# A two-layer graph attention kernel: the normalized input turned in 32 by 32 blocks on VectorE, and elu plus one with a single exponential

## The chip, the cores and the metric

The kernel runs on one core of a Trainium2 chip. The metric is the device time of one execution in microseconds (us), lower is better; where several runs were made it is their median. A core has five engines that run side by side, each through its own queue in a fixed order: TensorE (PE in the profile, with its weight loads as PEld), VectorE (DVE), ScalarE (ACT), GpSimd (POOL) and SyncE (SP), which here only issues DMAs. They wait for each other through semaphores. TensorE leaves its products in eight banks of its output memory (PSUM), which VectorE and ScalarE must empty ("drain").

## The reference

B = 32 batches, N = 512 nodes, 512 features, all in fp32; layer 1 has 4 heads of 256, layer 2 one head of 512.

```python
def gat_layer(x, mask, W, a_src, a_dst, bias, concat):
    xl = (x @ W).reshape(B, N, H, F)
    asrc = jnp.einsum('bnhf,hf->bnh', xl, a_src)
    adst = jnp.einsum('bnhf,hf->bnh', xl, a_dst)
    e = jax.nn.leaky_relu(asrc[:, :, None, :] + adst[:, None, :, :], NEG_SLOPE)
    e = jnp.where(mask[..., None], e, NEG_INF)
    attn = jax.nn.softmax(e, axis=1)
    out = jnp.einsum('bsdh,bshf->bdhf', attn, xl)
    out = out.reshape(B, N, H * F) if concat else out.mean(axis=2)
    return out + bias
...
mask = (adj > 0) | jnp.eye(N, dtype=bool)[None]
h = jnp.maximum(_layernorm(x, axis=-1), 0.0)
g = jax.nn.elu(gat_layer(h, mask, W1, att_src1, att_dst1, b1, concat=True))
return x + gat_layer(g, mask, W2, att_src2, att_dst2, b2, concat=False)
```

## The kernel before

`tile_gat` (L347) does not issue its work directly. It records jobs in a `Program` (from L101): each has an engine, a planned cost in us, and the keys it reads and writes. A list scheduler (`order`) then lays the jobs out. TensorE keeps the order in which the jobs were recorded; VectorE, ScalarE, GpSimd and SyncE are reordered by the planned costs and by what waits for a job. `emit` (L1525) issues the instructions in that order, so it is fixed before the kernel runs. All instructions pass through a few helpers, and so they share line numbers in the profile: `act` is L476, `dve` L479, `dma` on SyncE L482, GpSimd's adding DMA of the mask into `p` L487, `pe` L493; only SyncE's transposing DMAs have lines of their own, L637 (`mt<-m`) and L696 (`x<-adj`). Work is told apart by tile names.

The matrix products are done by a Strassen-Winograd scheme in seven half-size products instead of eight (`sevens`, L931, and `gather1`, L1146, for layer 1's weighted sum). Each product is named by a number n from 1 to 7, needs some sums of blocks on its left or right (VectorE: `hs<-ht`, `hs<-h`, `x<-xl`, `t<-p`), and leaves banks that are copied (ScalarE) or added (VectorE) into the result. A matrix product in fp32 takes two passes on TensorE.

A batch goes through these steps:

- `load` (L602) reads x in four tiles of 128 rows. `norm` (L645) takes mean and variance on VectorE. `norm_turn` (L665) does `x<-x,stats` (scale, shift and Relu in one ScalarE instruction) and turns the tile, since TensorE needs it with features on partitions (`ht`). For the first two batches TensorE turns it. For the 30 others ScalarE splits the fp32 words into 16-bit halves (`adj<-x`), SyncE issues a transposing DMA (`x<-adj`), and ScalarE puts the halves together (`ht<-x`).
- `project1` (L1028): `ht` times W1, as `mm<-w_sb,ht` and `mm<-w_sb,hs`, into `xl`, with the attention scores in extra columns.
- softmax of layer 1, over several steps: scores (`z`, `flip`), DMAs that spread them over partitions (`drr<-flip`, `rr<-drr`, `das<-flip`, `as<-das`), sums of exponentials (`l`, `low`), and `p`: VectorE writes it, GpSimd adds the mask (`p<-dm`), ScalarE takes the exponential (`p<-p,z`).
- `gather1` (L1146): `p` times `xl`, into `h`, transposed. The banks are copied into `h` by ScalarE (`h<-mm`) or added by VectorE. When a group is complete, `elu` (L1049) turns it into elu plus one, up to sign: ScalarE takes exp (`xr<-h,b_sb`), then a Relu (`xr<-xr`), and VectorE joins it with the bias (`h<-h,b_sb,xr`).
- `project2` (L1223): `h` times W2. Two of the seven products find `b2_sb` already in their banks, put there by ScalarE (`mm<-b_sb`).
- `gather2` (L1314), layer 2's weighted sum. `residual` reads x again (`t<-in_x_dram`) and the result leaves with `out_dram<-t`. Its sums on the right side (`sums2`, L1299) borrow two of the four x tiles.

The main loop (L1463) records for each batch i: `gather1` of batch i+1, heads 0 and 1; `project1` of batch i+2, first half; `gather1`, heads 2 and 3; `project1`, second half; `gather2` of batch i-1; `project2` of batch i+1; then `load`, `norm` and `norm_turn` of batch i+3. On TensorE the last two stand between each other's products where the recorder pairs them (`pipe`). Ahead of the loop, `weights2` (L555) loads W2, b1 and b2, and the first batches go through simpler versions (`project1_first`, `gather1_plain`, L1061).

Of the kernel before, what the change touches and what calls it, by code (L numbers as in the profile page):

```python
# [346 lines left out]
def tile_gat(  # L347
# [74 lines left out]
    AT = {(0, 0): 0, (0, 1): 6, (1, 0): 1, (1, 1): 2}  # L422
    b1_sb = sbuf.tile([P, 2, FT], F32, name="b1_sb")
    b2_sb = sbuf.tile([P, 2, W2H], F32, name="b2_sb")
    part = sbuf.tile([P, 2, FT, 2], F32, name="part")
    xl = sbuf.tile([P, NT, H, W], F32, name="xl")
# [4 lines left out]

    xs = slots("x", NT, [P, D])
    adj2 = sbuf.tile([P, 2, N], I32, name="adj2")
# [121 lines left out]
    def weights2():  # L555

        for (r, c), ix in AT.items():
            dma(
                1.5, [("ht", 0, 0)], [("w2", ix)], w2_sb[:, ix, :, :M],
                w2[r * HF // 2 : (r + 1) * HF // 2, c * DO // 2 : (c + 1) * DO // 2].rearrange(  # L560
                    "(k p) f -> p k f", p=P
                ),
            )
        dma(0.1, (), ["b1"], b1_sb[:, 0], b1.rearrange("(c p) -> p c", p=P))
        dve(TINY, ["b1"], ["b1"], nc.vector.tensor_scalar_mul, b1_sb[:, 1], b1_sb[:, 0], -1.0)
        dve(0.3, (), ["b2"], nc.vector.memset, b2_sb, 0.0)
        for c in range(2):
            dma(
                0.4, (), ["b2"], b2_sb[:, c, :M],
                bass.AP(tensor=b2.tensor, offset=b2.offset + c * M, ap=[[0, P], [1, M]]),  # L570
            )
        dve(0.34, ["b2"], ["b2"], nc.vector.tensor_sub, b2_sb[:, 1], b2_sb[:, 0], b2_sb[:, 1])
        dve(0.2, ["b2"], ["b2"], nc.vector.tensor_scalar_mul, b2_sb[:, 0], b2_sb[:, 0], -1.0)
        for a, v in enumerate((as2, ad2)):
            lk, bc = ts_.take()
            bc = bc[:, 0, :]
            dma(0.75, (), [lk], bc, rows_of(v[0], P))
            for (r, c), ix in AT.items():
                for k in range(KH):
                    jk, junk = xrs.take()  # L580
                    dve(
                        0.4, [lk, ("w2", ix)], [("part", a, r, c, k), jk],
                        nc.vector.scalar_tensor_tensor,
                        junk[:, : DO // 2], w2_sb[:, ix, k, :M], 1.0,
                        bc[:, c * DO // 2 : (c + 1) * DO // 2], op0=OP.mult, op1=OP.mult,
                        accum_out=part[:, a, r * KH + k, c : c + 1],
                    )
                    xrs.give(jk)
            ts_.give(lk)
        for a in range(2):  # L590
            for r in range(2):
                g = part[:, a, r * KH : (r + 1) * KH, :]
                dve(
                    TINY, [("part", a, r, c, k) for c in range(2) for k in range(KH)],
                    [("w2s", AT[r, a])], nc.vector.tensor_add,
                    w2_sb[:, AT[r, a], :, M:], g[:, :, 0:1], g[:, :, 1:2],
                )


    XT, MASK, MASKT, ST = {}, {}, {}, {}  # L600

    def load(b):  # L602
        XT[b] = []
        for t in range(NT):
            xk, xt = xs.take()
            dma(1.1, (), [xk], xt, x[b, t * P : (t + 1) * P, :])
            XT[b].append((xk, xt))

# [36 lines left out]
    def norm(b):  # L645
        sk, st = stats.take()
        S, A = nc.vector.BN_STATS_DIM, nc.vector.BN_AGGR_DIM
        for t, (xk, xt) in enumerate(XT[b]):
            dve(0.61, [xk], [sk + (t,)], nc.vector.bn_stats, st[:, t, :S], xt)
            dve(TINY, [sk + (t,)], [sk + (t,)], nc.vector.bn_aggr, st[:, t, S : S + A], st[:, t, :S])  # L650
# [14 lines left out]
    def norm_turn(b, t):  # L665

        (sk, st), (xk, hn) = ST[b], XT[b][t]
        S, A = nc.vector.BN_STATS_DIM, nc.vector.BN_AGGR_DIM
        act(
            0.71, [xk, sk + (t,)], [xk], hn, hn, AF.Relu,  # L670
            bias=st[:, t, S : S + 1], scale=st[:, t, S + A : S + A + 1],
        )
        if b < 2:
            pk, pt = banks.take()
            pe(
                [xk], [pk], 0.44,
                [(nc.tensor.transpose, (pt[:, k * P : (k + 1) * P], hn[:, k * P : (k + 1) * P], identf), {})
                 for k in range(KT)],
            )
            act(  # L680
                0.62, [pk], [("ht", t, 0), ("ht", t, 1)], ht[:, :, t * P : (t + 1) * P],
                pt.rearrange("p (k n) -> p k n", n=P), AF.Copy,
            )
            banks.give(pk)
        else:

            ak, a = adjs.take()
            words = a.bitcast(U16)
            act(
                0.96, [xk], [ak], words.rearrange("p (h f) -> p h f", h=2),  # L690
                hn.bitcast(U16).rearrange("p (f h) -> p h f", h=2), AF.Copy,
            )
            back = hn.bitcast(U16)
            prog.add(
                "SP", 1.3, [ak], [xk],
                lambda: nc.sync.dma_start_transpose(  # L696
                    back.rearrange("p (g n) -> p g n", n=P), words
                ),
                1.9,
            )  # L700
            act(
                1.21, [xk], [("ht", t, 0), ("ht", t, 1)],
                ht[:, :, t * P : (t + 1) * P].bitcast(U16).rearrange("p k (n h) -> p h k n", h=2),
                back.rearrange("p (h k n) -> p h k n", h=2, n=P), AF.Copy,
            )
            adjs.give(ak)
        xs.give(xk)
        if t == NT - 1:
            stats.give(sk)


    def p_keys(pk, us=range(NT), cs=range(2)):
# [195 lines left out]
    def ht_blocks():  # L908
        return half_blocks(ht, KQ, lambda r, c: [("ht", 2 * r, c), ("ht", 2 * r + 1, c)])

# [4 lines left out]

    def minus(to):

        def put(n, us, bks, ps, fresh):  # L920
            d, keys = to(us, *BLOCK[n - 1])
            if fresh:
                act(COPY2, bks, keys, d, ps, AF.Copy, scale=-1.0)
            else:
                dve(ADD2, bks + keys, keys, nc.vector.tensor_sub, d, d, ps)

# [72 lines left out]
    def project1_first(zt):  # L999

        for j in range(H // 2):
            zk, z = zt[j]
            for t in range(NT):
                for c in range(2):
                    h = 2 * j + c
                    bk, bt = banks.take()
                    pe(
                        [("ht", t, 0), ("ht", t, 1)]
                        + [q for r in range(2) for k in range(KQ)
# [18 lines left out]
    def project1(b, left, j):  # L1028
        def to(us, r, c):
# [6 lines left out]
        yield from sevens(  # L1036
            left, lambda n, u, k: w1_sb[:, n - 1, k, u[1], :], lambda n: w1_keys(n - 1), minus(to),
            KQ, [(m, j) for m in range(2)], W, LAST,
# [9 lines left out]

    def elu(g, places, at):  # L1049

        keys = [("h1", g, r) for r in range(2)]
        ek, e = xrs.take()
        act(0.62, [*places, "b1"], [ek], e, at, AF.Exp, bias=b1_sb[:, 0, g : g + 1], scale=-1.0)
        act(0.54, [ek], [ek], e, e, AF.Relu, bias=1.0, scale=-1.0)
        dve(
            0.65, [*places, ek, "b1"], keys, nc.vector.scalar_tensor_tensor,
            h1[:, g, :], at, b1_sb[:, 1, g : g + 1], e, op0=OP.add, op1=OP.min,
        )
        xrs.give(ek)

    def gather1_plain(soft, heads):  # L1061

        for h in heads:
            pk, p = soft.p.pop(h)
            for f in range(FPH):
                bk, ps = banks.take()
                for s in range(NT):
# [8 lines left out]
                    )  # L1076
                elu(h * FPH + f, [bk], ps)
                banks.give(bk)
            ps_.give(pk)
            yield h  # L1080
# [65 lines left out]
    def gather1(soft, order):  # L1146
# [11 lines left out]
        for u, n in order:  # L1158
# [27 lines left out]
            elif n in (2, 4, 5, 6):  # L1186
                act(COPY2 if two else COPY, bks, keys, to, ps, AF.Copy)
            else:
                dve(ADD2 if two else ADD, bks + keys, keys, nc.vector.tensor_add, to, to, ps)
            if n in (2, 3, 4):  # L1190
# [11 lines left out]
            if n in (3, 4):  # L1202
                for q in g:
                    elu(q, [("h1", q, x) for x in range(2)], h1[:, q, :])
            if n == 4:
# [17 lines left out]
    def project2(b, left, order=LAST):  # L1223
# [7 lines left out]
        def to(us, r, c):  # L1231
# [6 lines left out]
            left, lambda n, u, k: w2_sb[:, n - 1, k, :],  # L1238
            lambda n: [("w2", n - 1), ("w2s", n - 1)], minus(to), KH, [(0,), (1,)], W2H, order,
            {1: (b2_sb[:, 0], "b2"), 5: (b2_sb[:, 1], "b2")},  # L1240
        )

    def scores_2(b):
        def cols(z, i, zk):
            v = x2(b)
            for a in range(2):
                dve(
                    TINY, [x2_key(b, t, a) for t in range(NT)], [zk + (0, a)],
                    nc.vector.tensor_copy, z[:, a, 0, :], v[:, :, a * W2H + M],
                )  # L1250
# [35 lines left out]
    def sums2(b, soft, place=None, keys=None):  # L1286
# [12 lines left out]
        t1, t2 = (  # L1299
            (t.rearrange("p (k f) -> p k f", f=M), [k]) for k, t in (xs.take() for _ in range(2))  # L1300
        )
# [12 lines left out]
    def gather2(b, soft, blocks, order=LAST):  # L1314
# [27 lines left out]
        for n in (5, 6):  # L1342
            xs.give(right[n][1][0])

# [54 lines left out]
    S1, S2 = {}, {}  # L1399
    HT_KEYS = [("ht", t, c) for t in range(NT) for c in range(2)]  # L1400

# [35 lines left out]
    flush()  # L1437
    weights2()
    s = S1[1] = Soft(1, 1, scores_1)
    for h in gather1_plain(S1[0], range(H)):  # L1440
# [116 lines left out]
```

## Time and profile before

| what | value |
|---|---|
| median of 3 runs | 2822.73 us (2817.69 to 2825.91) |
| the profiled execution | 2826.34 us, its span 2824.6 us |
| granted TensorE clock, mean | 0.994 |
| GpSimd busy | 328.3 us (12%) |
| mean memory traffic | 178 GB/s |

The costliest groups of ScalarE, VectorE and GpSimd, by names: instruction, count, busy us and mean ns of one.

| group | count | busy us | mean ns |
|---|---|---|---|
| ACT `l<-l,low` | 640 | 454.5 | 712 |
| ACT `p<-p,z` 128x512 | 628 | 429.7 | 713 |
| ACT `xr<-h,b_sb` (exp of elu) | 248 | 171.8 | 714 |
| ACT `ht<-x` (halves put together) | 120 | 160.6 | 1351 |
| ACT `xr<-xr` (Relu of elu) | 256 | 153.9 | 620 |
| ACT `h<-mm` 128x512 | 240 | 140.4 | 585 |
| ACT `adj<-x` (words split) | 120 | 125.2 | 1046 |
| DVE `p<-rr,z` | 628 | 450.5 | 743 |
| DVE `h<-h,b_sb,xr` (elu) | 248 | 181.9 | 744 |
| DVE `flip<-low` 128x32 transpose | 161 | 33.1 | 206 |
| POOL `p<-dm` (adding DMA, issue) | 314 | 275.1 | 880 |

"Busy" is time in which an engine works on instructions; an idle gap stands in brackets with what ended it, as `[4.18 <-ACT p L476]`. In `out<-in` the names are those of the program's tiles (`mm` is a bank, `w_sb` all weights). SyncE's waits are those of its queue (SPq): while it waits for one DMA's inputs, the DMAs behind it wait as well.

### The profile page before, as it was taken

To read this page: it belongs to the slowest core of one execution; us is meant where nothing else is said; L and a number is where in the kernel's file an instruction comes from. 1 tells how busy PE (TensorE), PEld (TensorE's weight loads), DVE (VectorE), ACT (ScalarE), POOL (GpSimd) and SP (SyncE) were. 2 spreads that over 40 slices of the span, in tenths; PEclk is the share of its full clock that TensorE was granted. 3 is DMA by queue.
4 is the path that set the end of the run, shared out by engine and by line. 5 is a ranking of instruction groups with operands and counts; after the bars stand their busy time and mean duration, and the time that the engine had idled before them with its cause. 6 is when DMAs were issued, how large, how long until landed. Compare 5 with 4: busy or idle time off the path is not lost.

```text
span 2824.6 us, 39689 instructions
## 1 busy us (share of the span) xinstructions
PE 2763.9 (98%) x12524; PEld 2376.7 (84%) x12524; DVE 2432.9 (86%) x5526; ACT 2381.3 (84%) x4506; POOL 328.3 (12%) x356
## 2 busy tenths in 40 slices
PE   8899999999999999999999999999999999999998
PEld 6588888888888888888888888888888888888876
DVE  7788988898988888888889888888888898898885
ACT  5798888889889889888898888888888888888973
POOL 0100111110111111111101111011111011110110
PEclk9999999999999999999999999999999999999999
DMA  7575866666866666766668766687756776766763
GB/s 220 141 172 149 207 184 171 177 179 184 207 173 171 175 180 186 186 184 171 171 175 203 185 168 178 180 184 186 181 157 183 175 194 185 176 178 176 187 168 101
DMA packets 373831, 501.96 MB, mean 178 GB/s; under 512 B 220788, under 2 KB 225652, under 8 KB 373620
## 3 DMA queue, kind: packets, MB, share of 16 engines
q1 hardware_dynamic: 327828, 332.67, 42.3%
q0 software_dynamic: 45792, 166.74, 25.3%
q8 instruction: 99, 1.62, 0.2%
q14 instruction: 112, 0.92, 0.1%
HBM read 316.41 MB, written 51.31 MB: 130 GB/s over the span
## 4 chain that ended last, share of the span: by engine, by line
PE 49%; DMA 4%; ACT 3%; DVE 2%; issue 1%; ACTq 0%; DVEq 0%; POOLq 0%
PE mm L493 49%; DMA p<-dm 2%; ACT l L476 1%; DMA x<-adj 1%; DMA drr<-flip 1%; DVE p L479 1%; ACT p L476 0%; DMA rr<-drr 0%; ACT ht L476 0%; DVE hs L479 0%; DVE t L479 0%; ACT adj L476 0%; ACT xl L476 0%; ACT x L476 0%; ACT mm L476 0%
## 5 line engine op out<-in xcount | busy, mean ns | idle before, releaser
L493 PE MATMUL mm<-w_sb,hs 128*128 128x257 f32 (+2 forms) x3032 | 698.7, 381 | 15.7 <-DVE hs L479 10.7
L493 PEld LDWEIGHTS mm<-w_sb,hs 128*128 128x128 f32 x3032 | 573.5, 190 | 106.7 <-DVE hs L479 15.0
L487 POOL DMA_DIRECT2D p<-dm x314 | 275.1, 880 | 2336.4 <-DVE p L479 1053.9
L479 DVE CUSTOM_DVE_ANT_1 l<-l,mt 128x512 f32<-128x512 f32 x640 | 424.9, 685 | 131.2 <-ACT l L476 124.9
L476 ACT ACTIVATE p<-p,z 128x512 f32<-128x512 f32 (+1 forms) x636 | 433.4, 711 | 122.2 <-DMA p<-dm 100.6
L493 PE MATMUL mm<-w_sb,ht 128*128 128x258 f32 x2112 | 502.0, 382 | 5.2 <-DVE xl L479 2.1
L493 PE MATMUL mm<-p,xl 128*128 128x256 f32 (+1 forms) x1984 | 478.6, 384 | 1.9 <-ACT xr L476 0.8
L479 DVE SCALAR_TENSOR_TENSOR p<-rr,z 128x512 f32<-128x512 f32 (+1 forms) x636 | 454.0, 740 | 30.8 <-DMA rr<-drr 28.2
L476 ACT ACTIVATE l<-l,low 128x512 f32<-128x512 f32 x640 | 454.5, 712 | 20.5 <-DVE low L479 19.8
L476 ACT ACTIVATE l<-as,z 128x512 f32<-128x512 f32 x640 | 434.8, 711 | 37.7 <-DMA as<-das 36.8
L493 PE MATMUL mm<-w_sb,h 128*128 128x257 f32 x2048 | 459.0, 381 | 5.3 <-ACT mm L476 4.1
L493 PEld LDWEIGHTS mm<-w_sb,ht 128*128 128x128 f32 x2112 | 401.7, 190 | 65.0 <-DVE xl L479 3.2
L493 PEld LDWEIGHTS mm<-w_sb,h 128*128 128x128 f32 x2048 | 389.5, 190 | 65.3 <-ACT mm L476 5.3
L493 PEld LDWEIGHTS mm<-p,xl 128*128 128x128 f32 x1984 | 378.6, 191 | 63.0 <-issue 6.5
L493 PE MATMUL mm<-xl,p 128*128 128x256 f32 (+1 forms) x1024 | 249.2, 386 | 4.4 <-DVE t L479 2.3
L476 ACT ACTIVATE xl<-mm 128x514 f32<-128x514 f32 (+2 forms) x380 | 222.2, 585 | 35.9 <-PE mm L493 33.8
L493 PE MATMUL mm<-t,hs 128*128 128x256 f32 x992 | 234.2, 382 | 7.3 <-ACT mm L476 6.3
L493 PEld LDWEIGHTS mm<-xl,p 128*128 128x128 f32 x1024 | 193.1, 189 | 40.5 <-issue 5.8
L493 PEld LDWEIGHTS mm<-t,hs 128*128 128x128 f32 x992 | 188.0, 191 | 37.6 <-ACT mm L476 9.6
L476 ACT ACTIVATE xr<-h,b_sb 128x512 f32<-128x512 f32 x248 | 171.8, 714 | 24.4 <-DVE h L479 20.4
L479 DVE SCALAR_TENSOR_TENSOR h<-h,b_sb,xr 128x512 f32<-128x512 f32 x248 | 181.9, 744 | 9.9 <-ACT xr L476 9.5
L476 ACT ACTIVATE h<-mm 128x512 f32<-128x512 f32 (+1 forms) x256 | 146.4, 572 | 30.1 <-PE mm L493 29.5
(110 smaller groups left out, 3206.9 us busy)
## 6 DMA issues: line engine op xcount, KB each, us to landing
p<-dm POOLq DMA_DIRECT2D x314, 512.0 KB, 5.6
rr<-drr SPq DMA_DIRECT2D x159, 512.0 KB
x<-in_x_dram SPq DMA_DIRECT2D x128, 256.0 KB
adj<-in_adj_dram SPq DMA_DIRECT2D x128, 256.0 KB
as<-das SPq DMA_DIRECT2D x64, 512.0 KB
t<-in_x_dram SPq DMA_DIRECT2D x62, 512.0 KB
out_dram<-t SPq DMA_DIRECT2D x60, 512.0 KB
dm<-m SPq DMA_DIRECT2D x64, 256.0 KB
```

The costliest lines, as they stand in the source:

```text
L476: prog.add("ACT", cost, reads, writes, lambda: nc.scalar.activation(*a, **k))
L479: prog.add("DVE", cost, reads, writes, lambda: f(*a, **k))
L487: lambda: nc.gpsimd.dma_start(to, at, accum_op=OP.add), size,
L493: f(*a, **k)
```

## The change

Three things are changed.

*Turning x.* For batches 2 to 31 the split, the transposing DMA and the merge are gone. The x load is laid out otherwise: DMA t puts 128 consecutive rows of x on 32 partitions with four rows each, so that every tile holds every fourth row on its partitions. After scale, shift and Relu of all four tiles, VectorE transposes 32 by 32 blocks (`turn`, four instructions of 128x512), into the two `adj` tiles and into parts of the x tiles. Then 32 small DMAs on SyncE carry the blocks, 32 partitions by 2 by 128 words each, to their places in `ht`. Each piece of `ht` has its own key. The batches 0 and 1 are loaded and turned as before.

*Elu plus one.* With y the weighted sum and b its bias, elu(y+b)+1 is the larger of min(exp(y+b), 1) and y+b+1. The first copy from a bank into `h` now adds b+1 and turns the sign (ScalarE, Identity with bias, 256 columns at a time since the bias differs by group); `elu` is then one exp on ScalarE and one VectorE instruction. The Relu is gone. The sign of `h` is the other one, so additions and subtractions in the drains are exchanged.

*The one taken back.* The column sums of W2 are subtracted from b2 once: `bias2` multiplies a tile of ones with all blocks of W2 on TensorE (16 products, after `weights2` and ahead of the first `gather1_plain`), and VectorE subtracts the result from `b2_sb`, which ScalarE puts into the banks of `project2` as before. What falls on the two score columns is kept in `c2` and added by `scores_2`.

In the order of instructions, TensorE has these 16 more and is otherwise unchanged; ScalarE has 3620 instead of 3868, VectorE 5588 instead of 5464, SyncE 2012 instead of 1172, GpSimd 361 in both.

```diff
-        dve(TINY, ["b1"], ["b1"], nc.vector.tensor_scalar_mul, b1_sb[:, 1], b1_sb[:, 0], -1.0)
+        dve(TINY, ["b1"], ["b1"], nc.vector.tensor_scalar_add, b1_sb, b1_sb, 1.0)
...
-        dve(0.34, ["b2"], ["b2"], nc.vector.tensor_sub, b2_sb[:, 1], b2_sb[:, 0], b2_sb[:, 1])
-        dve(0.2, ["b2"], ["b2"], nc.vector.tensor_scalar_mul, b2_sb[:, 0], b2_sb[:, 0], -1.0)
...
+    def bias2():
+        ok, ones = ts_.take()
+        ones = ones[:, 0, :P]
+        dve(0.2, (), [ok], nc.vector.memset, ones, 1.0)
+        for c in range(2):
+            bk, bt = banks.take()
+            pe(
+                [ok, *(k for r in range(2) for k in (("w2", AT[r, c]), ("w2s", AT[r, c])))],
+                [bk], 2 * KH * W2H / 593,
+                [
+                    (mm, (bt[:, :W2H], ones, w2_sb[:, AT[r, c], k, :]),
+                     dict(start=(r == 0 and k == 0), stop=(r == 1 and k == KH - 1)))
+                    for r in range(2) for k in range(KH)
+                ],
+            )
+            dve(ADD, [bk, "b2"], ["b2"], nc.vector.tensor_sub, b2_sb[:, c], b2_sb[:, c], bt[:, :W2H])
+            banks.give(bk)
+        dve(TINY, ["b2"], ["c2"], nc.vector.tensor_copy, c2, b2_sb[:, :, M])
+        dve(0.34, ["b2"], ["b2"], nc.vector.tensor_sub, b2_sb[:, 1], b2_sb[:, 1], b2_sb[:, 0])
...
     def load(b):
+        XT[b] = sorted(((k, t) for k, t in (xs.take() for _ in range(NT))), key=lambda kt: kt[0])
+        for t, (xk, xt) in enumerate(XT[b]):
+            if b < 2:
+                dma(1.1, (), x_keys(xk), xt, x[b, t * P : (t + 1) * P, :])
+            else:
+                dma(
+                    1.1, (), [xk + (t,) for xk, _ in XT[b]], xt4[t * Q : (t + 1) * Q],
+                    x[b, t * P : (t + 1) * P, :].rearrange("(t r) f -> r t f", t=NT),
+                )
...
     def norm_turn(b, t):
-            ak, a = adjs.take()
-            words = a.bitcast(U16)
-            act(
-                0.96, [xk], [ak], words.rearrange("p (h f) -> p h f", h=2),
-                hn.bitcast(U16).rearrange("p (f h) -> p h f", h=2), AF.Copy,
-            )
-            back = hn.bitcast(U16)
-            prog.add(
-                "SP", 1.3, [ak], [xk],
-                lambda: nc.sync.dma_start_transpose(
-                    back.rearrange("p (g n) -> p g n", n=P), words
-                ),
-                1.9,
-            )
-            act(
-                1.21, [xk], [("ht", t, 0), ("ht", t, 1)],
-                ht[:, :, t * P : (t + 1) * P].bitcast(U16).rearrange("p k (n h) -> p h k n", h=2),
-                back.rearrange("p (h k n) -> p h k n", h=2, n=P), AF.Copy,
-            )
...
+            if b > 1:
+                turn(b)
+
+    def turn(b):
+        every = [q for xk, _ in XT[b] for q in x_keys(xk)]
+        ks = [adjs.take()[0] for _ in range(2)]
+        flat = adj2.bitcast(F32).rearrange("p a n -> p (a n)")
+        low = xt4[:, :, : D // 2]
+        for k in range(KT):
+            c, kk = divmod(k, KQ)
+            into = xt4[:, :, k * P : (k + 1) * P].rearrange("p t (j f) -> p j t f", f=Q)
+            if c == 0:
+                to, keys = flat[:, kk * N : (kk + 1) * N], [ks[kk]]
+                reads, keys = every, [*keys, ("low", kk)]
+            else:
+                to = low[:, 2 * kk : 2 * kk + 2, :]
+                reads, keys = [*every, ("low", 0), ("low", 1)], [("turned", kk)]
+            dve(0.59, reads, keys, nc.vector.transpose, to, into)
+        for c in range(2):
+            for i in range(NT):
+                for j in range(NT):
+                    at = slice(i * Q, (i + 1) * Q)
+                    if c == 0:
+                        came, keys = flat.rearrange("p (k j n) -> p j k n", k=KQ, j=NT)[at, j], ks
+                    else:
+                        came = low[at].rearrange("p (k u) (v n) -> p u v k n", u=2, v=2)[:, j // 2, j % 2]
+                        keys = [("turned", 0), ("turned", 1), *every]
+                    dma(
+                        0.2, keys, [("ht", i, c, j)],
+                        ht[j * Q : (j + 1) * Q, c * KQ : (c + 1) * KQ, i * P : (i + 1) * P], came,
+                        0.35,
+                    )
...
     def elu(g):
-        act(0.62, [*places, "b1"], [ek], e, at, AF.Exp, bias=b1_sb[:, 0, g : g + 1], scale=-1.0)
-        act(0.54, [ek], [ek], e, e, AF.Relu, bias=1.0, scale=-1.0)
+        act(0.62, keys, [ek], e, h1[:, g, :], AF.Exp, bias=-1.0)
         dve(
-            h1[:, g, :], at, b1_sb[:, 1, g : g + 1], e, op0=OP.add, op1=OP.min,
+            h1[:, g, :], e, 1.0, h1[:, g, :], op0=OP.min, op1=OP.max,
         )
...
     def gather1_plain(soft, heads):
-                elu(h * FPH + f, [bk], ps)
+                act(
+                    0.54, [bk, "b1"], [("h1", g, r) for r in range(2)], h1[:, g, :], ps, AF.Identity,
+                    bias=b1_sb[:, g : g + 1], scale=-1.0,
+                )
                 banks.give(bk)
+                elu(g)
...
     def gather1(soft, order):
             elif n in (2, 4, 5, 6):
-                act(COPY2 if two else COPY, bks, keys, to, ps, AF.Copy)
+                for i, q in enumerate(g):
+                    act(
+                        COPY, [bks[i], "b1"], [keys[i]], h1[:, q, c * M : (c + 1) * M], ps[:, i, :],
+                        AF.Identity, bias=b1_sb[:, q : q + 1], scale=-1.0,
+                    )
             else:
-                dve(ADD2 if two else ADD, bks + keys, keys, nc.vector.tensor_add, to, to, ps)
+                dve(ADD2 if two else ADD, bks + keys, keys, nc.vector.tensor_sub, to, to, ps)
...
     def scores_2(b):
-                nc.vector.tensor_copy, z[:, a, 0, :], v[:, :, a * W2H + M],
+                nc.vector.tensor_scalar_add, z[:, a, 0, :], v[:, :, a * W2H + M], c2[:, a : a + 1],
...
     weights2()
+    bias2()
     s = S1[1] = Soft(1, 1, scores_1)
```

## The prediction

> **What bounds the kernel now.** I read the page's first part, then the list of what TensorE waits for, then busy time by stretch, then TensorE's timeline where that table shows loss, and last the chain of waits around one stall.
>
> ```profile
> PE 2763.9 (98%) x12524; PEld 2376.7 (84%) x12524; DVE 2432.9 (86%) x5526; ACT 2381.3 (84%) x4506; POOL 328.3 (12%) x356
> ...
> PE mm L493 <- ACT mm L476: 13.8, 14, 3.9
> PE mm L493 <- DVE hs L479: 10.7, 9, 2.2
> ```
>
> TensorE is the bound. VectorE and ScalarE have some 400 us spare each, so 400 us taken from ScalarE buys only the moments when TensorE stands still. All waits in that list add up to 57 us; that is the whole field of play on the side of gains.
>
> ```profile
> 0.00:85.00 85.00, 68.78 (x282) 54.41 (x283) 67.14 (x258) 46.27 (x95) 8.34 (x14) 0.91 0.81 223
> 85.00:170.00 85.00, 77.07 (x277) 54.02 (x276) 67.70 (x161) 71.32 (x132) 10.81 (x11) 0.95 0.61 152
> 170.00:2720.00 2550.00, 2525.96 (x11591) 2198.22 (x11590) 2232.19 (x4976) 2217.08 (x4184) 302.25 (x323) 1.00 0.69 179
> 2720.00:2824.00 104.00, 92.11 (x378) 70.07 (x377) 65.86 (x136) 46.63 (x98) 6.94 (x8) 1.00 0.41 119
> ```
>
> Columns: stretch, length, busy time of TensorE, its weight loads, VectorE, ScalarE and GpSimd, granted clock, DMA share, GB/s. Thirty batches in the long stretch lose 24 us together, 0.8 us in a batch of 85. The first 170 us lose 24 us idle, and clock besides. Startup:
>
> ```profile
> 73.91 2.01 PE L493 MATMUL mm<-w_sb,ht 128*128 128x258 f32 x8 [1.26 <-DVE xl L479]
> 80.10 8.43 PE L493 MATMUL mm<-p,w_sb 128*128 128x512 f32 x12 [4.18 <-ACT p L476]
> ...
> 117.88 6.62 PE L493 MATMUL mm<-w_sb,h 128*128 128x257 f32 x16 [3.90 <-ACT mm L476]
> ...
> 150.52 1.99 PE L493 MATMUL mm<-t,hs 128*128 128x256 f32 x8 [1.70 <-ACT mm L476]
> ```
>
> [...] 16 passes of 257 columns take 6.62 us here and 3.5 where TensorE is warm (0.217 a pass). One steady stall, from the chain of waits and TensorE's timeline:
>
> ```profile
> 1169.19 8.68 DMA p<-dm
> ...
> 1178.58 1.33 ACT ht L476
> ...
> 1179.94 0.70 DVE hs L479
> ...
> 1180.68 2.67 PE L493 MATMUL mm<-w_sb,hs 128*128 128x258 f32 x8 [2.21 <-DVE hs L479]
> ```
>
> An `ht` copy on ScalarE queues behind an exp that waits for the mask's DMA; VectorE's sum of `ht` blocks follows it, and TensorE waits. Eight such stalls in the steady part make some 10 us.
>
> [...] SyncE waited 554.1 us in 148 waits for VectorE's `flip`. [...] Before has only the 128x32 form, 0.205 us, so the large one is unseen.
>
> **The change part by part.** Counts are from the two instruction lists, durations from the groups of before.
>
> *ScalarE loses work.* Removed: 120 word splits `adj<-x` at 1.046 us (125), 120 merges `ht<-x` at 1.351 (161), 256 Relus `xr<-xr` (154): 440 us. The bank copies `h<-mm` (240 of 128x512 at 0.585, 16 of 128x256, 146 us in all) become 496 of 128x256 at about 0.38 and 8 wide ones (193): +47. The net is about −395 us, 13 in each batch; ScalarE falls from 84% to some 70%. None of it is on TensorE's path by itself. What it buys is that nothing queues behind the exp of the mask. The `ht<-x` step of the eight stalls no longer exists (−10), and of the 9.6 us that TensorE waits in the steady part for ScalarE's `mm`, `xl` and `p` I expect about two thirds to go (−6): −16. Bounds: 0, if VectorE is late in its place, to −20.
>
> *VectorE gains work.* 120 transposes of 128x512. The nearest rows are a 128x512 add at 0.685 and statistics at 0.683[...]. I take 0.69, +83 us; from 0.6 to 1.2 (the price of a 1024-wide add) it is 72 to 144. VectorE goes from 86% to about 90%, hidden as long as its queue is not late in the stretch below. The elu keeps its one operation of 0.744. Drains that change a subtraction into an addition, or back, cost nothing.
>
> *Turning x: from 4 DMA transposes a batch to 32 plain DMAs.* SyncE loses 120 transposes (1.3 us of issue each) and gains 960 DMAs of 32 KB, 64 pieces of 512 B, beside four-way split x loads in the same number as before. I bound the issue pitch by neighbours: 0.33 (`rr<-drr`, `x` loads), 0.38 to 0.40 (`out_dram<-t`, `as<-das`), 0.52 (`drr<-flip`), plus some 0.09 between issues: 0.42 to 0.61. I take 0.47, so 15 us for 32.
> They can be hidden or not, by this timetable of one batch (TensorE times of before). Relu of the last x quarter ends about 1248.3; the first two transposes follow on VectorE until 1250.4, and the first DMA goes at 1250.5. The blocks that the first sum of `ht` reads are complete with the 24th DMA, with one `drr` for the softmax (0.6) among them: 1250.5 + 24 x 0.47 + 0.6 = 1262.4, landing some 1.3 later (as between a `drr` and the `rr` that needs it): 1263.7. In before, this sum ran at 1264.35. TensorE wants its result at 1267.45, and wants VectorE's later drain of the gather's last banks at 1269.19; between lie the four sums, one `xl`, two `p` and two drains, some 6 us. So it is just met, with 0 to 0.6 us of stall. I charge 0.33 in each of 30 batches: +10. Bounds: 0 (pitch 0.42) and +94 (pitch 0.60: 3.1 us late, 30 times). The other SyncE traffic is moved as well: `drr`, `rr`, `adj` and `out` issues after the burst's start stand up to a few DMAs later, and x loads now wait for all four slots, two of them held by gather2's sums; their next use is a batch away, which covers it.
>
> *DMA engines.* They lose the transposes' small packets, most of the 220788 under 512 B, so `p<-dm` (5.6 us to landing, for which ScalarE waits 100.6 us) may land sooner. No row prices that; I take 0, between −5 and +3.
>
> *Bias matmuls.* 32 passes of 257 columns at 0.217: 7.0 us, placed in TensorE's order just where the 4.18 gap is. Column 0 needs W2's row products, which VectorE has done by then (its first 16 precede the `p` that the gap waits for), so 16 passes fill 75.9 to 79.4; the second 16 run to 82.9; then the 16 passes of 512 run warm (7.0) instead of 8.43 + 0.78 + 1.98, and end at 89.9 where before they ended at 91.1: −1.2. Bound: +7 if W2 or its products are late and the gap stays.
>
> *Startup seeds.* At 117.88 ScalarE's seed waits for a bank that exp, Relu and VectorE must leave; now one Identity frees it. The gap falls from 3.90 to about 1.9 (−2.0), and with that short a gap the 16 passes take 3.5 rather than 6.62 (−3.1). The 1.70 gap at 150.52 loses about 1. Startup together: −1.2 − 2.0 − 3.1 − 1 = −7; range −9 to +8.
>
> *Tail.* Of the 12 us idle after 2720, 4.4 lie behind ScalarE's `h` and weight copies; half goes: −2.
>
> *Sum.* −7 − 16 + 10 − 2 = −15. Against the profiled execution (2826.3, its span 2824.6) that is 2811.3; this execution lies 3.6 above the median 2822.7 of three runs, so the median to expect is 2807.7, rounded to **2808**.
>
> **The rivals.**
> - *The burst is late (slower).* Place: VectorE's first `ht` sum in each batch. Price: every 0.01 us of pitch above 0.47 moves it by 0.24 us; at 0.55 it is 1.9 us in 30 batches, 58 us, in place of my 10: 2808 + 48 = **2856**. It decides from a pitch of about 0.50. For it: 0.52 measured for `drr`, and 0.44 to 0.56 even for plain `x` and `rr` issues under load. Against it: 64 pieces are fewer than the 128 of an x load at 0.33.
> - *Nothing to gain.* The stalls change their owner (VectorE at 90% is late for `hs` where ScalarE was), and the 7 us of bias passes eat the startup's gain: **2822**.
> - *Most stalls go.* The burst is early enough, 22 of the steady part's 24 us go, startup −7, tail −4: −33, **2790**.
>
> **How the numbers follow.** Forecast 0.40, late burst 0.28, nothing 0.18, most stalls 0.14. About 0.3%, 8.5 us, can be told from no change. Faster: 0.34 of the forecast's, the 0.14 and 0.03: 0.51. Same: 0.05 of the forecast and 0.13 of the nothing case: 0.18. Slower: 0.28, with the ends of the forecast and of the nothing case, 0.03: 0.31. The range runs from 2788, which takes in nearly all of the last case, to 2852, about the middle of the late burst; outside it lie 0.06 below and 0.14 above. The likeliest case's own range is 2795 to 2822.
>
> **What would show it.** ScalarE near 1985 us busy; the large transpose at 0.69; SyncE's issues of `ht` with a spacing of 0.47; no wait of VectorE's `hs` for ScalarE's `ht`, and in its place short waits for the DMA into `ht`; the 4.18 gap filled. If TensorE's waits for `hs` pass 1 us in most batches, the burst is late. The prediction is wrong if TensorE's pass time itself changes, or if the `p` DMAs, past which the burst moves much traffic, land later.

## The result: 12% slower, and the profile after

The changed kernel took 3165.48 us (median of 4 runs, 3161.62 to 3172.47) against 2820.51 before (4 runs in the same comparison): ratio 1.1223, 95% interval 1.1195 to 1.1252. That is 345 us, or 11.5 us in each of the 30 batches whose x is turned by VectorE. It lies far outside the range; the rival "the burst is late" names the right cause, but at 2856 it has only a tenth of the loss. The profiled execution has a span of 3165.9 us. The first part of its page, and the list of what TensorE waits for (us, times, longest):

```profile
PE 2886.4 (91%) x12556; PEld 2440.0 (77%) x12556; DVE 2490.4 (79%) x5650; ACT 2062.0 (65%) x4258; POOL 321.2 (10%) x356
```

```profile
PE mm L495 <- DMA ht<-adj: 133.1, 29, 6.3
PE mm L495 <- ACT xl L478: 61.5, 30, 4.0
PE mm L495 <- DVE xl L481: 28.4, 19, 5.3
PE mm L495 <- DVE h L481: 20.0, 13, 6.8
```

Two things are to be seen. TensorE now stands for 280 us, and the largest part waits, once in nearly every batch, for the DMAs that carry the turned blocks into `ht`. And TensorE is *busy* for 122 us more than before, although it has only the 16 bias products more to do, 32 passes in the trace (12556 less 12524) and 7.1 us. The stretch of the 30 batches tells why; columns as in the prediction:

```profile
170.00:3060.00 2890.00, 2644.97 (x11598) 2257.36 (x11598) 2292.83 (x5104) 1913.07 (x3957) 296.04 (x324) 0.96 0.59 159
```

The granted clock is 0.96 where it was 1.00: after the long stalls a row of passes runs slow (8 of them in 3.78 us below, where 1.90 is usual). One batch shows it all, in the timeline of SyncE's queue, of VectorE and of TensorE (start, duration, instruction, count, and in brackets the idle time before it):

```profile
1393.57 0.33 SPq L484 DMA_DIRECT2D rr<-drr  x1
1401.13 3.92 SPq L484 DMA_DIRECT2D ht<-adj  x6
1405.15 0.58 SPq L484 DMA_DIRECT2D ht<-x  x1
1405.83 0.57 SPq L484 DMA_DIRECT2D drr<-flip  x1
1406.46 4.48 SPq L484 DMA_DIRECT2D ht<-x  x7
1410.99 8.58 SPq L484 DMA_DIRECT2D ht<-adj  x10
1419.62 0.58 SPq L484 DMA_DIRECT2D rr<-drr  x1
1420.24 5.08 SPq L484 DMA_DIRECT2D ht<-x  x8
1425.42 0.56 SPq L484 DMA_DIRECT2D das<-flip  x1
```

```profile
1399.81 1.30 DVE L481 STREAM_TRANSPOSE adj<-x 128x512 f32<-128x512 f32 x2
...
1417.96 0.69 DVE L481 TENSOR_TENSOR hs<-ht 128x512 f32<-128x512 f32 x1 [7.07 <-DMA ht<-adj]
```

```profile
1414.59 1.89 PE L495 MATMUL mm<-p,xl 128*128 128x256 f32 x8
1421.07 3.78 PE L495 MATMUL mm<-w_sb,ht 128*128 128x258 f32 x8 [4.59 <-DMA ht<-adj]
1424.65 2.28 PE L495 MATMUL mm<-w_sb,hs 128*128 128x258 f32 x8
```

The 32 DMAs of one batch hold SyncE for 24 us, not 15. The first 24 are issued 18.4 us after the first, and TensorE's product starts 1.5 us after that; it was wanted at 1416.5, where the product ahead of it ends. VectorE stands for 7.07 us in front of one sum, with everything that is queued behind it. The 8 passes after the stall take 3.78 us where 1.90 is usual. And the softmax's `rr` DMA goes 13.8 us after the `drr` ahead of it, with 17 `ht` DMAs in between; in the batch of before that the timetable was taken from, it was 1.7 to 4.3 us. One view gives the price of one such DMA (shortest, median and longest issue in ns):

```profile
L484 SPq DMA_DIRECT2D ht<-adj x480: 585/595/2056, 133.7 to 2981.2; - x160
L484 SPq DMA_DIRECT2D ht<-x x480: 585/595/2263, 142.1 to 2986.9; - x160
```

0.595 us, and about 0.05 to the next: a pitch of 0.64 where nothing disturbs it (8 DMAs in 5.08 us above). Some take up to 2.3 us: the whole burst above, 34 issues with the softmax's two, takes 24.2 us, 0.71 for each. The expectations below reckon with 0.67, between the two. The order of all queues was laid out with a planned cost of 0.35 us, the last number in the diff of `turn`.

### The profile page after: what moved, and what is told of

The parts are those of the page before. It is cut to its first block, busy times and chain, and to the rows that moved or that the text cites. A ratio compares the mean times of both kernels' runs of the same rounds, so it can differ in the third digit from the quotient of the medians.

```text
span 3165.9 us, 40828 instructions
## 1 busy us (share of the span) xinstructions
PE 2886.4 (91%) x12556; PEld 2440.0 (77%) x12556; DVE 2490.4 (79%) x5650; ACT 2062.0 (65%) x4258; POOL 321.2 (10%) x356
## 5 line engine op out<-in xcount | busy, mean ns | idle before, releaser
L495 PE MATMUL mm<-w_sb,hs 128*128 128x257 f32 (+2 forms) x3032 | 733.6, 394 | 49.1 <-ACT xl L478 23.5
L495 PEld LDWEIGHTS mm<-w_sb,hs 128*128 128x128 f32 x3032 | 596.7, 198 | 157.3 <-DVE h L481 28.6
L495 PE MATMUL mm<-w_sb,ht 128*128 128x258 f32 x2112 | 562.0, 415 | 165.9 <-DMA ht<-adj 133.1
L495 PEld LDWEIGHTS mm<-w_sb,ht 128*128 128x128 f32 x2112 | 431.2, 207 | 254.6 <-issue 127.2
L495 PE MATMUL mm<-p,xl 128*128 128x256 f32 (+1 forms) x1984 | 485.9, 388 | 7.1 <-ACT p L478 5.6
L478 ACT ACTIVATE xr<-h 128x512 f32<-128x512 f32 x256 | 154.1, 624 | 308.6 <-DVE h L481 297.2
L478 ACT ACTIVATE h<-mm,b_sb 128x256 f32<-128x256 f32 (+1 forms) x504 | 224.0, 471 | 144.9 <-PE mm L495 142.0
L481 DVE SCALAR_TENSOR_TENSOR h<-xr,h 128x512 f32<-128x512 f32 x256 | 172.3, 684 | 49.8 <-ACT xr L478 49.7
```

The lines of the kernel that those rows point to most:

```text
L478: prog.add("ACT", cost, reads, writes, lambda: nc.scalar.activation(*a, **k))
L481: prog.add("DVE", cost, reads, writes, lambda: f(*a, **k))
L495: f(*a, **k)
```

## The experiments

Theory A: the burst on SyncE, longer than planned, is the whole loss. Rival B: the elu part has a share. Rival C: the transposes, the four-way loads and the new order of the queues lose time whatever the DMAs cost. All ratios are to runs of the kernel before on the same chip, with 95% intervals; differences in us between two experiments are of medians, in part from different chips, on which the kernel before took 2820 to 2824 us.

### One part alone

e1 keeps the elu part and the bias matmuls and turns x as before; e2 does the opposite.

```diff
 e1
-            if b < 2:
+            if True:
...
+            ak, a = adjs.take()
...
-            if b > 1:
-                turn(b)
...
 e2
-        act(0.62, keys, [ek], e, h1[:, g, :], AF.Exp, bias=-1.0)
+        act(0.62, [*places, "b1"], [ek], e, at, AF.Exp, bias=b1_sb[:, 0, g : g + 1], scale=-1.0)
+        act(0.54, [ek], [ek], e, e, AF.Relu, bias=1.0, scale=-1.0)
...
-    bias2()
```

> Only the elu part and the bias matmuls; x is loaded and turned as before. If the DMA burst of the turn is the whole loss (theory A), this part alone loses nothing and gains what the prediction gave it: 2800 to 2822 us, ScalarE near 2110 us busy. If the elu part carries a share of the loss (rival B: two Identity copies of 0.47 us in place of one copy of 0.585 hold the banks longer), it is above 2860.

Measured: 2849.61 us, ratio 1.0084 (1.0056 to 1.0112). Neither case: the elu part is not neutral, it loses some 26 us. ScalarE is busy for 2299.1 us and not near 2110: the splits and merges of words, 286 us of its work, stay in this run.

> Only the turn by VectorE and the 32 DMAs per batch; elu as before. Theory A: all of the loss is here, 3150 to 3200 us. Rival B: clearly below 3120.

Measured: 3127.12 us, 1.1076 (1.1041 to 1.1112). Between the two cases: some 304 us of the loss are in the turn, and B has a small share.

### Taking the burst away

e3 leaves the `ht` jobs out, so the planner makes a new order. e5 keeps the jobs, and with them the order of every queue, but issues nothing for them.

```diff
 e3
+                    if c == 0 or c == 1:
+                        continue
                     dma(
 e5
-                    dma(
-                        0.2, keys, [("ht", i, c, j)],
-                        ht[j * Q : (j + 1) * Q, c * KQ : (c + 1) * KQ, i * P : (i + 1) * P], came,
-                        0.35,
-                    )
+                    prog.add("SP", 0.35, keys, [("ht", i, c, j)], lambda: None, 0.2)
```

> The changed kernel without the 960 DMAs that carry the turned blocks into ht, so batches 2 to 31 project an old ht; transposes, x loads and all else stay. Theory A (SyncE's queue, 0.67 us per DMA): the loss goes, 2790 to 2830 us. Rival C (the loss lies in VectorE's added transposes, the four-way x loads and the new order of the queues): 2950 us or more stays.

Measured: 2904.80 us, 1.0281 (1.0242 to 1.0319). Between the two again. Since the order is another one here, the run can't say whether the 80 us that stay belong to the work or to the order.

> The changed kernel with every queue in its own order, laid out as if the 960 ht DMAs were there, but these DMAs are not issued (batches 2 to 31 project an old ht). Theory A1: the loss comes from the burst being longer on the chip (0.67 us a DMA) than the order was laid out for (0.35), so without it the order is good: 2800 to 2850 us. Theory A2: the order itself is bad whatever the DMAs cost: 2900 us or more, as in the run without these jobs (2905).

Measured: 2863.88 us, 1.0160 (1.0135 to 1.0185), just above A1's case and clearly below A2's. With the same order, the DMAs are worth 301 of the 345 us. TensorE's longest waits in e5, and the busy time of all engines over its span:

```profile
PE mm L495 <- ACT xl L478: 29.2, 15, 3.5
PE mm L495 <- ACT mm L478: 24.8, 23, 3.0
```

```profile
sum 2867.00, PE 2778.65 PEld 2382.76 DVE 2479.37 ACT 2055.82 POOL 323.69; mean PE 926.22 PEld 794.25 DVE 826.46 ACT 685.27 POOL 107.90
```

TensorE is busy for 2778.65 us; with the DMAs it was 2886.4. So of the 299 us between the two profiled spans, 108 are slow passes and 191 are standing still, of which only 133 wait for `ht` itself. This late burst cost over twice the 133.1 us that TensorE waits for it.

### How long the burst may be

e9 keeps the order too and issues every second `ht` DMA, so that the burst is about as long as planned. e8 issues all, with half the pieces in each.

```diff
 e9
+    def hold(size, reads, writes, to, at, cost):
+        prog.add("SP", cost, reads, writes, lambda: None, size)
...
-                    dma(
+                    ship = dma if (i + j) % 2 else hold
+                    ship(
...
 e8
-                        ht[j * Q : (j + 1) * Q, c * KQ : (c + 1) * KQ, i * P : (i + 1) * P], came,
+                        ht[j * Q : (j + 1) * Q, c * KQ : c * KQ + 1, i * P : (i + 1) * P], came[:, :1],
```

> The changed kernel with all queues in its own order, every second ht DMA not issued (half of ht stays old): 16 DMAs at 0.67 us take 10.7 us, about what the order was laid out for (32 at 0.35 us, 11.2 us). If the loss comes from the burst being longer than planned (theory A1), nearly all of it goes: 2860 to 2900 us, near the run without any of these DMAs (2864). If it grows with the number of DMAs and of bytes, in proportion, it is half way: about 3015.

Measured: 2882.09 us, 1.0215 (1.0188 to 1.0242): as theory A1 says. Half of the DMAs cost 18 us more than none, the second half 283 more. The price is not proportional; this fits a price that begins where the burst outlasts what the order gives it.

> The changed kernel, in the same order, each ht DMA with 32 pieces of 512 B in place of 64: half of every second block of ht stays old. If the issue of a DMA costs a fixed time, it stays at 0.59 us and the kernel at 3150 to 3180 us; if it is paid by the piece, it falls towards 0.3 to 0.4 us and the kernel below 3000.

Measured: 3133.38 us in a single run, a little below the first case and far from the second. The view of the `ht` DMAs settles it:

```profile
L484 SPq DMA_DIRECT2D ht<-adj x480: 507/589/1607, 129.7 to 2945.1; - x160
```

32 pieces take 0.589 us where 64 took 0.595. So with half the pieces and half the bytes the issue of one of these DMAs is only 0.006 us shorter in the median, and nearly the whole loss stays; fewer DMAs (e9, 2882.09 us) or a second queue (e13, 2916.11) take most of it away.

### Telling the planner the price

e4 gives the planner 0.66 us for an `ht` DMA. e7 also puts every second one on GpSimd's queue (`other`). e10 and e11 are these two with two more planned costs set to the traces' values.

```diff
 e4
-                        0.35,
+                        0.66,
 e7
-                    dma(
+                    put = other if (i + j) % 2 else dma
+                    put(
...
-                        0.35,
+                        0.9 if (i + j) % 2 else 0.66,
 e10, e11: also
-                            2.5, keys + [mk + (us[0] // 2,)], keys,
+                            3.8, keys + [mk + (us[0] // 2,)], keys,
...
-                        COPY, [bks[i], "b1"], [keys[i]], h1[:, q, c * M : (c + 1) * M], ps[:, i, :],
+                        0.42, [bks[i], "b1"], [keys[i]], h1[:, q, c * M : (c + 1) * M], ps[:, i, :],
```

> The changed kernel with the planned cost of one ht DMA raised from 0.35 to 0.66 us, what its issue takes in the trace; the planner may then lay the queues out otherwise. If most of the loss is a wrong order (softmax DMAs behind the burst), the time falls below 3000 us; if it is the burst's own length (21 us between the end of the Relus and the first sum of ht), it stays above 3080 us.

Measured: 2947.81 us, 1.0437 (1.0403 to 1.0470). One number in the plan, and the order that came of it, take 218 us off, with every DMA still issued on one queue at the same 0.595 us. TensorE's wait for `ht<-adj` falls from 133.1 to 27.2 us:

```profile
PE mm L495 <- DMA ht<-adj: 27.2, 16, 2.9
```

> The changed kernel with every second ht DMA on GpSimd's queue (planned at 0.9 us) and the others on SyncE's at 0.66. If the length of the burst on one queue is what remains of the loss in the run with the corrected price (2948), two queues take it from 21 to about 14 us and the time falls to 2850 to 2910; if the mask DMAs of GpSimd, which now stand behind ht DMAs, are late instead, it is 2950 or above.

Measured: 2923.53 us, 1.0374 (1.0346 to 1.0401): 24 us better, and somewhat short of the first case's range. GpSimd issues such a DMA in 0.536 us.

> The changed kernel with three planned costs set to what the traces show: 0.66 us for an ht DMA, 0.42 for an Identity copy, and 1.3 us more for the mask's adding DMA (issue to landing 5.25 us planned instead of 3.95; the traces have 5.1 to 5.6). With only the first of them it took 2948, and ScalarE waited 239 us for the mask's DMA. If these waits are what is left of a wrong order, it falls to 2850 to 2900; if SyncE's burst itself is what is left, it stays within 20 us of 2948.

Measured: 3025.59 us, 1.0718 (1.0687 to 1.0750), in neither case.

> As the run before, with every second ht DMA on GpSimd's queue (planned at 0.9 us). If burst and mask waits add up, this is the best with the turn: 2820 to 2880. If GpSimd's mask DMAs then stand behind ht DMAs, it is no better than the one on SyncE alone.

Measured: 3094.58 us, 1.0962 (1.0933 to 1.0992), worse still, as in the second case. ScalarE waits only 46.6 us for the mask's DMA here, so late mask DMAs are not shown to be the reason. My idea that ScalarE's waits for this DMA are the rest of the loss fell: in e10 they did fall, from 239 us in e4, but the order made with the new price kept TensorE waiting for the exp and for what follows it:

```profile
ACT p L478 <- DMA p<-dm: 74.8, 48, 3.9
```

```profile
PE mm L495 <- DVE t L481: 57.1, 38, 3.0
PE mm L495 <- ACT p L478: 50.7, 27, 3.3
PE mm L495 <- ACT h L478: 36.4, 30, 1.8
```

So three planned costs that are nearer to the traces than e4's one gave an order that is 78 us worse: right prices alone do not make a good order.

### The same order, a shorter burst, everything computed

e13 is e5 and e9 with nothing left out: the order is that of the changed kernel, but every second `ht` DMA is issued by GpSimd at its place. e14 and e15 are e5 and e13 for the turn alone. e16 is e5 with the Identity copies planned at 0.42 us, as in e10.

```diff
 e13, e15
+    def aside(size, reads, writes, to, at, cost):
+        prog.add("SP", cost, reads, writes, lambda: nc.gpsimd.dma_start(to, at), size)
...
-                    dma(
+                    ship = aside if (i + j) % 2 else dma
+                    ship(
```

> The changed kernel with every queue in its own order, planned as before (0.35 us a DMA, all on SyncE), but every second ht DMA is issued by GpSimd at that place of its queue. Each queue then has 16 DMAs, some 10 us, which is what was planned. If the burst's length beyond its plan is the cause, a kernel that computes everything falls to 2870 to 2920 us; if GpSimd's mask DMAs come late behind them, or the 32 DMAs cost in the DMA engines, it is above 2980.

Measured: 2916.11 us, 1.0329 (1.0305 to 1.0354), in the first case's range. A complete kernel wins back 249 of the 345 us by the second queue alone. TensorE now waits 7.3 us for `ht<-adj`:

```profile
PE mm L498 <- DMA ht<-adj: 7.3, 5, 3.1
```

> The turn part alone (elu as before), in the order of that kernel, with the ht DMAs not issued (old ht in batches 2 to 31). The same with the elu part took 2864. If the 41 us that are left there come from the elu part (which alone costs 26 at its planned price), this is 2815 to 2845; if they come from the turn's order, in which ScalarE waits twice as long for the mask's DMA, 2850 to 2880.

Measured: 2834.21 us, 1.0053 (1.0038 to 1.0068): the first case. Transposes, four-way loads and new order cost the turn 14 us; rival C is nearly out.

> The turn part alone with every second ht DMA issued by GpSimd, order and planned costs kept: a complete kernel. If burst and elu part add up, 2830 to 2880 us, some 20 to 40 below the run with both parts; if the elu part has no share, it is within 15 us of that run.

Measured: 2894.80 us, 1.0267 (1.0250 to 1.0284), above the first case's range, though 21 us below e13. So the elu part keeps its share, and half of the burst on each queue still costs the turn 61 us over e14. In its waits, 20.4 us are for `ht<-adj` and 29.8 for VectorE's `h`.

> Both parts, ht DMAs planned at 0.35 us but not issued, with the planned cost of an Identity copy 0.42 us in place of 0.28, and so a new order. If the mispriced copy is what the elu part costs (26 us alone, 5 when priced right), it falls from 2864 to 2835 to 2850; if order luck decides, it lies anywhere from 2840 to 2900, not below.

Measured: 2858.32 us, 1.0129 (1.0110 to 1.0148), above the first case and inside the range that luck of the order was given. Beside the turn, the copies' right price gives 6 us, and the intervals of e16 and e5 overlap, so even this is not clear of noise.

### The elu part

e6 is e1 with the copies planned at 0.42 us, e12 also with the longer mask DMA.

```diff
 e6, e12
-                        COPY, [bks[i], "b1"], [keys[i]], h1[:, q, c * M : (c + 1) * M], ps[:, i, :],
+                        0.42, [bks[i], "b1"], [keys[i]], h1[:, q, c * M : (c + 1) * M], ps[:, i, :],
...
 e12: also
-                            2.5, keys + [mk + (us[0] // 2,)], keys,
+                            3.8, keys + [mk + (us[0] // 2,)], keys,
```

> The elu part alone, with the planned cost of the two Identity copies 0.42 us instead of 0.28; the trace shows 0.84 for a pair. If the elu part alone is slower (2850) because the order was laid out with too small a price for these copies, this one falls to 2805 to 2830; if it is by the work itself or by the luck of one order, it stays at 2840 or more.

Measured: 2829.27 us, 1.0023 (1.0009 to 1.0038). This is at the upper end of the first case: with the right price, and the order that came of it, some 20 us of e1's loss go. Each price was run in one order only, so price and luck of the order are not told apart.

> The elu part alone with the planned costs 0.42 us for an Identity copy and 1.3 us more for the mask's DMA. If the elu part's small loss (2829 with the first of these) is a matter of the order, it is 2800 to 2820, at or below the kernel before; if its gain is eaten by the bias products and the copies, 2825 to 2845.

Measured: 2824.18 us, 1.0012 (0.9998 to 1.0026): between the cases, just below the second, and not to be told from the kernel before. Here the mask's right price does no harm. ScalarE waits 3.5 us for the mask's DMA where it waits 76.5 in e6, and the time is only some 5 us less, so these waits of ScalarE cost little here. No version that I ran is faster than the kernel before.

## Why the prediction was wrong

*What bounds the kernel.* Right. The one engine without slack decided; 319 us less work on ScalarE bought nothing.

*The step that failed: "I take 0.47, so 15 us for 32".* The pitch is 0.64, and 0.71 in the mean of the burst shown, above even the upper bound of 0.61. That bound came from the nearest row, `drr<-flip` at 0.52, without room above it. None of the neighbours moves data from SBUF to SBUF, but no run shows whether that makes the price. Nor were the neighbours' rows prices for a burst: an `rr` DMA takes SyncE 0.33 us when nothing stands ahead of it and 0.58 right behind an `ht` DMA (1393.57 and 1419.62 above; medians of 69 and of 30 in this trace). But an `ht` DMA takes 0.69 even at the head of a burst (median of 29); what its price is made of stays open. The argument against the rival ("64 pieces are fewer than the 128 of an x load") was wrong in kind: in e8 32 pieces take 0.589 us, and 64 take 0.595.

The start of the timetable was good: the first DMA goes 1.8 us after the last Relu (2.2 in the prediction). The prediction gives no working for the end of that Relu, so that it is right may be luck. The deadline was wrong. The timetable asks when VectorE's sum of `ht` blocks is wanted (1267.45), but in the kernel before, the product ahead of that one reads `ht` itself:

```profile
1265.71 1.90 PE L493 MATMUL mm<-w_sb,ht 128*128 128x258 f32 x8
1267.45 1.90 PE L493 MATMUL mm<-w_sb,hs 128*128 128x258 f32 x8
```

This product is what stalls, and it, not the sum, needs the 24th DMA: it starts with its landing in 25 of the 30 batches, while the first sum mostly starts after the 19th (median). The sign "TensorE's waits for `hs` pass 1 us" therefore never came: TensorE waits for `hs` 0.5 us in all. With this deadline the arithmetic comes out. In the batch shown the 24 DMAs and the `drr` take 18.4 us where the prediction has 24 x 0.47 + 0.6 = 11.9, so they are 6.5 us late; 2.0 of them were slack (1265.7 less 1263.7), which leaves 4.5, and TensorE stood for 4.59. Of the 6.5 us, 4.1 are the pitch (24 x 0.17), and most of the rest are two DMAs in the burst that took 1.6 and 1.9 us.

*The second failure: the price of a late burst.* The rival charged the lateness once in each batch. Measured are 10 us a batch (301 in 30, by e5). The direct wait is 4.4 of them (133 in 30). Another 3.6 (108 in 30) are slow passes after stalls. The prediction has that double price for a gap of the startup (16 passes in 6.62 us after 3.90 us of waiting, 3.5 elsewhere) and does not use it here, though it names a change of TensorE's pass time as a sign of being wrong, and that sign came. Not every gap has it; it goes with the length of the stall: in the long stretch of the changed kernel's trace the first 8 passes after a stall take 2.01 us when it was under 2 us, 2.97 after 2 to 3 us, and 3.78 after 4 us and more (medians of 31, 14 and 27). The remaining 1.9 are further stalls: e5 has 58 us fewer of them, the `xl` drains of ScalarE and the `xl` and `h` drains of VectorE above all, which follow VectorE's 7 us in front of one sum and the softmax DMAs behind the burst. That these two are the channels is read from the trace; no run took one of them away alone.

*What I did not look at: the price that the order was made with.* The diff says 0.35 us for a DMA. Even my own 0.47 was above it, so the queues were laid out for a burst of 11 us that I myself put at 15. e4 shows what that means: 218 us for one planned number and the order made with it.

*ScalarE's load.* Predicted near 1985 us, measured 2062.0. A 128x256 Identity takes 0.47 us, not 0.38 (0.42 when two follow each other), 224 us for all instead of 193. The larger part is overlap. Added up one by one, ScalarE's instructions fall from 2777 to 2400 us, by 377, near the 395 of the prediction. But neighbouring instructions overlap a little, busy time counts the overlap once (2381.3 before, 2062.0 now), and it falls by only 319.

*VectorE.* Right: the large transpose takes 0.69 to 0.70 us, and the engine, 79% busy, is no bound. The drains `h<-h,mm`, with the sign exchanged, take 0.679 us where they took 0.680. But VectorE takes its queue in order, so its 7.07 us wait in front of one sum holds up the drains behind it.

*Steady gain of 16 us for ScalarE's stalls.* One reading in it was low: TensorE's waits for ScalarE's `mm`, `xl` and `p` in the long stretch of before are 11.9 us (7.7, 3.6 and 0.6), not 9.6. The `ht` step did vanish: TensorE waits 0.5 us for `hs` where it waited 10.7. But nothing came of it. With only the elu part, e12's TensorE stands for 19 us of the long stretch (2548 less 2528.76) where it stood for 24, and the runs do not show a gain. With only the turn and no burst, e14, it stands for 28. ScalarE, freed, waits at the mask's DMA instead, 180 us in e14 and 213 in e5 against 100.6 before, with bank drains queued behind.

*Startup.* Half right. The bias products fill the 4.18 gap and the seed's gap goes, with its slow passes:

```profile
80.77 7.12 PE L495 MATMUL mm<-w_sb,t 128*128 128x257 f32 x32
...
116.24 3.64 PE L495 MATMUL mm<-w_sb,h 128*128 128x257 f32 x16
```

But a new gap of 4.40 us behind a ScalarE bank copy opens at 68 us, so the bias products start 4.9 us later than I had them. The first gather of the loop starts at 141.97 instead of 145.21: −3.2, where I had −7.

*DMA engines, mask DMA.* Right to take 0: it lands after 5.1 us instead of 5.6.

*What stays open.* Priced right and alone, the elu part costs 5 us (e6) or nothing that is clear of noise (e12); beside the turn it costs some 24 to 30 (e16 and e5 less e14). That ScalarE, freed, then stands at the mask's DMA is a cause the traces suggest, but no run shows it: e12 took nearly all of these waits away and gained some 5 us, and the two runs that priced this DMA otherwise beside the turn got worse orders. Nor is it shown where the 52 us come from that e13 takes more than e5.

## What to carry to other kernels

When a change puts many small DMAs on one queue, the number to find first is the measured issue time of one of that kind (0.595 us here, where the neighbours' rows had 0.33 to 0.52). Take it from DMAs that stand behind others: an `rr` DMA that stands alone takes 0.33 us here, one behind an `ht` DMA 0.58. If no row of the trace has it, the upper bound has to leave room above the nearest row. Then look for the first instruction that reads the data itself, not only for sums made from it. Where instructions are ordered by planned costs, compare every planned cost in the diff with the trace: too low a price there doesn't just leave an estimate off, it can build the stall into the order, as e4 shows. A right price is no promise of a better order (e10), so each order has to be measured. And the long stall of TensorE that recurs in every batch costs more than its length here: after the 4.59 us of waiting shown, 16 passes take 5.9 us where they take 3.6 in before (1265.71 to 1269.35). Stalls under 2 us mostly cost just themselves here (8 passes in 2.01 us after them, where 1.90 is usual): e10's TensorE stands for 201 us, in many short stalls, but is busy for only 48 us more than in e5.

## What the runs showed of the hardware

A DMA of 32 partitions by 2 by 512 B from SBUF to SBUF takes SyncE 0.595 us to issue, with half the pieces 0.589, and GpSimd 0.536 (e7); x loads with eight times the bytes take 0.42 in the same kernel. What stands ahead counts: an `rr` DMA takes SyncE 0.33 us alone and 0.58 right behind an `ht` DMA. A pair of 128x256 Identity instructions with a bias takes 0.84 us, against 0.585 for one plain copy of 128x512. The 32 by 32 block transpose of 128x512 takes 0.69 to 0.70 us, an addition of that size 0.684 (`xl<-xl`).
